# A graph-attention kernel projects raw rows in layer 0, with its loads and its first graph cast reordered

## The chip, the core and the metric

The kernel runs on one core of one Trainium2 chip, as one launch. The metric is the device time in microseconds, shown as the median of several runs. The profile is one execution, recorded by the hardware profiler. Engines are called PE (TensorE), DVE (VectorE), ACT (ScalarE), POOL (GpSimd) and SP (SyncE); SP, ACT and POOL also issue DMAs, each into its own queue.

## The reference

There are two layers, and each adds a graph attention and then a feed-forward part to `x` (3327 rows of 256). Only layer 0's attention is touched by the change; the rest is a mixture of experts, a second attention, and thirty steps of a recurrent block. The attention of layer 0 is, with two heads of 128 columns:

```python
def _L0_gnn_ref(h, adj, W1, b1, W2, b2, W3, b3, a):      # h = layernorm(x)
    W1h = (h @ W1.T + b1).reshape(n, HEADS, C)
    W2h = (h @ W2.T + b2).reshape(n, HEADS, C)
    W3h = (h @ W3.T + b3).reshape(n, HEADS, C)
    a1, a2 = (a[:, :C], a[:, C:])
    s1 = jnp.einsum('nhc,hc->nh', W1h, a1)
    s2 = jnp.einsum('nhc,hc->nh', W2h, a2)
    e = jax.nn.leaky_relu(s1[:, None, :] + s2[None, :, :], ALPHA)
    e = jnp.where(adj[:, :, None] == 1, e, NEG)
    att = jax.nn.softmax(e, axis=1)
    return jnp.einsum('ijh,jhc->ihc', att, W3h).reshape(n, HEADS * C)
```

The graph `adj` is a 3327 x 3327 array of 32-bit integers.

## The kernel before

**Row tiles.** `x` lies in SBUF as 26 tiles of 128 rows. `groups` holds them by four (the last group by two): groups 0 to 6. SP loads one group with each of its first six DMAs of 512 KB (L76), and the last group in three pieces.

**Score weights.** The scores need W1 and W2 only through their products with the attention vector, two columns for each head. These are made once on PE (L415) and copied into the last four columns of `wv`, behind W3 (L419). So one 260-wide product gives both the projection and the scores. The biases' share of the scores, `shift`, comes from two more kinds of small products (L427). W1, W2, the attention vector (`gaT`), the biases and W3 are all loaded by POOL (L400, L412). ACT starts by issuing four DMAs that write zeros into DRAM tables (L393 to L396: `lists`, two rows of `given`, `no_row`).

**Projection.** `project` goes over the groups. For each it takes the statistics of the rows on DVE (L115, L116, L118), the power -1/2 on POOL (L120), and normalizes the rows on DVE (L127, into `xn`). By pairs of tiles, `turned` transposes on PE (L147) and copies to `hT` on ACT (L148); the products with `wv` follow one pair later (L162). `split0` adds the biases (L434, L438) and after each group `Scores.finish` takes three exponentials on ACT (L194 to L196). `project` has a second way, `raw=True`, used by layer 1: rows are turned as they are, the mean is taken out of the weights by `without_mean`, and the factor 1/std is applied to each row's result.

**The graph.** `take_graph` has POOL cast a group of graph rows from integers to one byte each, DRAM to DRAM, into the buffer `in_bytes` (L301), and SP turn them into `adjT` by DMA transposes (L311). `in_bytes` is one buffer, so the next cast waits for these transposes. The first cast is for four row tiles (`groups0[0]`), the later ones for six or four. The kernel places it after the power of group 3:

```python
def first_rows(ts, power):
    nonlocal behind
    behind = power
    if ts is groups[3]:
        take_graph(groups0[0], behind)
```

**Attention.** `attend` walks over parts of row tiles and heads. PE spreads a row factor over the partitions (L221), ACT copies it to `rb` (L225). For each of the 26 neighbour tiles ACT makes `e` (L252), DVE applies the mask to give `pT` (L257), and PE adds the product with `wh` into `acc` (L262).

**Order.** The order of instructions on an engine comes from a scheduler, which follows data dependencies and its own costs. `tc.issue_after(i)` places instructions behind `i`, and `tc.keep_in_program_order` keeps an instruction's place. [...]

Of the kernel before, what the change touches and what calls it, by code (L numbers as in the profile page):

```python
# [11 lines left out]
F32 = mybir.dt.float32  # L12
# [8 lines left out]
P = 128  # L21
# [9 lines left out]
def gat_moe_gat_recurrent_ffn(ctx: ExitStack, tc: tile.TileContext, a: dict, out: bass.AP):  # L31
# [59 lines left out]
            if REST % 2:  # L91
                move(dram[base + REST - 1 : base + REST, :], tile[REST // 2 : REST // 2 + 1, last, :])

    for ts in groups:
        move_pairs(a["x"], x[:, ts[0] : ts[-1] + 1, :], ts[0] // 2, (ts[-1] + 1) // 2, False)

    ident = const.tile([P, P], F32, name="ident")
    make_identity(nc, ident)
# [24 lines left out]
    def normalized(src, dst, scale=1.0):  # L123

        r, mv, power = inverse(src, scale)
        for j in range(len(src)):
            nc.vector.tensor_scalar(  # L127
                dst[j], src[j], mv[:, j, 0:1], r[:, j : j + 1], op0=ALU.subtract, op1=ALU.mult
            )
        return power  # L130

    def without_mean(wv, n_out, ones, p):

        for k in range(KD):
            nc.tensor.matmul(p[:, :n_out], lhsT=ones, rhs=wv[:, k, :], start=(k == 0), stop=(k == KD - 1))
        for k in range(KD):
            nc.vector.scalar_tensor_tensor(
                wv[:, k, :], p[:, :n_out], -1.0 / D, wv[:, k, :], op0=ALU.mult, op1=ALU.add
            )

    def turned(two, work, ps):

# [5 lines left out]
        nc.scalar.copy(hT, pt)  # L148
        return hT

    def project(groups, wv, n_out, finish, work, ps, ps_p, aside, raw=True):

        pending = None

        def products(hT, t, r):
            for j in range(2):
                p = ps_p()  # L160
                for k in range(KD):
                    nc.tensor.matmul(  # L162
                        p[:, :n_out], lhsT=hT[:, j, k, :], rhs=wv[:, k, :], start=(k == 0), stop=(k == KD - 1)
                    )
                finish(t + j, p, *([r[:, j : j + 1]] if raw else []))

        for ts in groups:
            n = len(ts)
            tiles = [x[:, t, :] for t in ts]
            if raw:  # L170
                r, _, power = inverse(tiles)
            else:
                xn = work.tile([P, G, D], F32, name="xn")
                power = normalized(tiles, [xn[:, j, :] for j in range(n)])
            aside(ts, power)
            for j0 in range(0, n, 2):
                hT = turned(x[:, ts[j0] : ts[j0] + 2, :] if raw else xn[:, j0 : j0 + 2, :], work, ps)
                if pending:
                    products(*pending)
                pending = hT, ts[j0], r[:, j0 : j0 + 2] if raw else None  # L180
        products(*pending)

    class Scores:


        def __init__(self, pool, heads, s=None):
            self.s = pool.tile([P, NT, 2, heads], F32, name="s") if s is None else s
            self.row = pool.tile([P, NT, heads], F32, name="row")
            self.full = pool.tile([P, NT, heads], F32, name="full")
            self.part = pool.tile([P, NT, heads], F32, name="part")  # L190
            self.minus = pool.tile([P, NT, heads], F32, name="minus")

        def finish(self, t0, t1):
            nc.scalar.activation(self.full[:, t0:t1], self.s[:, t0:t1, 1], AF.Exp)  # L194
            nc.scalar.activation(self.part[:, t0:t1], self.s[:, t0:t1, 1], AF.Exp, scale=ALPHA)
            nc.scalar.activation(self.row[:, t0:t1], self.s[:, t0:t1, 0], AF.Exp, scale=1.0 - ALPHA)  # L196
            nc.vector.tensor_scalar(self.minus[:, t0:t1], self.part[:, t0:t1], -1.0, None, op0=ALU.mult)

    quick = []
# [158 lines left out]
    with ExitStack() as moe:  # L358
# [17 lines left out]
        C = D // H  # L376
        keep = moe.enter_context(tc.tile_pool(name="keep0", bufs=1))
        wh = keep.tile([P, NT, H, C + 1], F32, name="wh")
        sc = Scores(keep, H)
        ps = moe.enter_context(tc.tile_pool(name="ps0", bufs=4, space=PSUM))  # L380
        ps_o = moe.enter_context(tc.tile_pool(name="ps0o", bufs=2, space=PSUM))
        nc.vector.memset(wh[:, :, :, C : C + 1], 1.0)
# [4 lines left out]
        with ExitStack() as pre:  # L387
            work = pre.enter_context(tc.tile_pool(name="work0", bufs=2))
            hold = pre.enter_context(tc.tile_pool(name="hold0", bufs=1))

            zero = hold.tile([P, E * CAP * 2 // P], F32, name="zero")
            nc.vector.memset(zero, 0.0)
            nc.scalar.dma_start(lists.rearrange("(p n) k -> p (n k)", p=P), zero)  # L393
            for k in range(2):
                nc.scalar.dma_start(given[k * NP + N : (k + 1) * NP, :], zero[: NP - N, :D])
            nc.scalar.dma_start(no_row, zero[:2, : NP // 4])  # L396

            def once(name, shape, src):
                t = hold.tile(shape, F32, name=name)
                nc.gpsimd.dma_start(t, src)  # L400
                return t

            w1 = once("gw1", [P, H, D], a["W1"].rearrange("(h c) d -> c h d", c=P))
            w2 = once("gw2", [P, H, D], a["W2"].rearrange("(h c) d -> c h d", c=P))
            aT = once("gaT", [P, 2, H], a["aT"].rearrange("(s c) h -> c s h", c=P))
            b1 = once("gb1", [P, H], a["b1"])
            b2 = once("gb2", [P, H], a["b2"])
            b3 = once("gb3", [P, D], every_partition(a["b3"], D))


            wv = hold.tile([P, KD, D + 2 * H], F32, name="wv")
            nc.gpsimd.dma_start(wv[:, :, :D], a["W3T"].rearrange("(k p) c -> p k c", p=P))  # L412
            pv = bank()
            for q, (s, h, k) in enumerate((s, h, k) for s in range(2) for h in range(H) for k in range(KD)):
                nc.tensor.matmul(  # L415
                    pv[:, q : q + 1], lhsT=(w1, w2)[s][:, h, k * P : (k + 1) * P], rhs=aT[:, s, h : h + 1],
                    start=True, stop=True,
                )
            nc.vector.tensor_copy(  # L419
                wv[:, :, D:].rearrange("p k q -> p q k"), pv[:, : 2 * H * KD].rearrange("p (q k) -> p q k", k=KD)  # L420
            )
            shift = hold.tile([P, 2, H], F32, name="shift")
            nc.vector.memset(shift, 0.0)
            pv = bank()
            for h in range(H):
                for s, b in ((0, b1), (1, b2)):
                    nc.tensor.matmul(  # L427
                        pv[:, h : h + 1], lhsT=b[:, h : h + 1].to_broadcast([P, P]), rhs=aT[:, s, h : h + 1],
                        start=(s == 0), stop=(s == 1),
                    )  # L430
            nc.vector.tensor_copy(shift[:, 0, :], pv[:, :H])

            def split0(t, p):
                nc.vector.tensor_tensor(  # L434
                    wh[:, t, :, :C], p[:, :D].rearrange("p (h c) -> p h c", h=H),
                    b3.rearrange("p (h c) -> p h c", h=H), ALU.add,
                )
                nc.vector.tensor_tensor(  # L438
                    sc.s[:, t], p[:, D : D + 2 * H].rearrange("p (s h) -> p s h", h=H), shift, ALU.add
                )  # L440
                if t % G == G - 1 or t == NT - 1:
                    sc.finish(t - t % G, t + 1)

            behind = None

            def first_rows(ts, power):
                nonlocal behind
                behind = power  # L450
                if ts is groups[3]:
                    take_graph(groups0[0], behind)

            project(groups, wv, D + 2 * H, split0, work, ps, bank, first_rows, False)
            nc.vector.tensor_scalar(wh[:, NT - 1], wh[:, NT - 1], real[:, 0:1], None, op0=ALU.mult)
            for ts in groups0[1:3]:
                behind = take_graph(ts, behind)


            nc.gpsimd.dma_start(gw, a["gate_w"].rearrange("(k p) e -> p k e", p=P))  # L460
            nc.gpsimd.dma_start(gb[:, 0, :], every_partition(a["gate_b"], E))

            def numbers(dst, pattern, base, step):
                nc.gpsimd.iota(
                    dst, pattern=pattern, base=base, channel_multiplier=step, allow_small_or_imprecise_dtypes=True
                )

            numbers(part, [[0, 1]], 0, 1)
            numbers(rank[:, 0, :], [[-1, E]], E, 0)
            numbers(region[:, 0, :], [[CAP, E]], 0, 0)  # L470
            for k in range(2):
                numbers(pair[:, :, k, 0], [[P, NT]], k * NP, 1)
            nc.gpsimd.affine_select(
                out=before, in_=ones, pattern=[[1, P]], compare_op=ALU.is_gt, fill=0.0, base=0, channel_multiplier=-1
            )
# [620 lines left out]
```

The softmax here doesn't subtract the row's maximum and nothing guards it: scores larger than these inputs give would overflow.

## Time and profile before

| | |
|---|---|
| Median of 3 runs | 1968.25 us (1965.48 to 1968.59) |
| Profiled execution, its own time | 1964.56 us |
| Span in the profile | 1962.6 us |
| Busy: PE / DVE / ACT / POOL | 1908.9 / 1281.6 / 1096.5 / 936.5 us |
| Mean granted PE clock | 0.994 |

The span is the time from the first to the last recorded instruction; the execution's own time holds some 2 us more around it. The busy time of an engine is the sum over its instructions, and a busy PE is not necessarily a PE at its peak rate. In the timeline each row is one instruction or a run of equal ones: start in us, length in us, engine, line, what it writes and reads, and in brackets the idle time of the engine before it, with what ended that. An engine name with a q (SPq, ACTq) is the issue of a DMA.

### The profile page before, as it was taken

What the parts mean: (1) busy time and instruction counts of PE and PEld (TensorE: products, weight loads), DVE (VectorE), ACT (ScalarE), POOL (GpSimd) and SP (SyncE); (2) the same over time, 40 slices, a digit from 0 to 9 for tenths busy, and PEclk for the clock granted to TensorE, in tenths of its full rate; (3) what the DMA queues carried; (4) which work ended last, traced back from release to release, by engine and by line L of the source; (5) the groups of instructions that cost most, each with busy time, mean ns of one, the idle gap of its engine ahead of it and who ended that gap; (6) DMA issues with size and microseconds to landing.
All of it is one profiled execution on the core that took longest, in us unless ns stands there. A gap on an engine that the chain in (4) does not pass through costs nothing.

```text
span 1962.6 us, 33704 instructions
## 1 busy us (share of the span) xinstructions
PE 1908.9 (97%) x12032; PEld 1747.3 (89%) x12032; DVE 1281.6 (65%) x3827; ACT 1096.5 (56%) x1509; POOL 936.5 (48%) x864
## 2 busy tenths in 40 slices
PE   7999999999999997999999999999999999999998
PEld 6999999998999995888888888888888888888887
DVE  6887788832222225566767777777777777777778
ACT  2977766721111113666555666666666666666664
POOL 3020202353333322010000488878888887888886
PEclk9999999999999998999999999999999999999999
DMA  8978051099999874000000000000000000000003
GB/s 168 117 104 118 6 86 50 18 307 303 357 326 336 280 245 148 2 15 9 17 9 17 28 1 1 1 1 1 1 1 1 1 1 1 1 1 1 1 1 118
DMA packets 139756, 157.09 MB, mean 80 GB/s; under 512 B 52028, under 2 KB 99365, under 8 KB 139587
## 3 DMA queue, kind: packets, MB, share of 16 engines
q1 hardware_dynamic: 123466, 122.05, 20.1%
q0 software_dynamic: 11440, 28.09, 8.3%
q10 hardware_dynamic: 4680, 4.76, 0.7%
q8 instruction: 98, 1.61, 0.3%
q14 instruction: 72, 0.58, 0.1%
HBM read 164.58 MB, written 29.78 MB: 99 GB/s over the span
## 4 chain that ended last, share of the span: by engine, by line
PE 71%; issue 9%; POOL 5%; DVE 4%; DMA 3%; ACT 1%; SPq 0%; POOLq 0%; DVEq 0%; ACTq 0%
PE po L1024 35%; PE acc L262 24%; PE pt L1008 8%; POOL given L831 2%; DVE pT L257 2%; POOL rb L730 2%; DMA given<-wh,to 2%; PE bank L786 1%; PE bank L499 1%; DMA wh<-in_w_dram 1%; DMA lists<-pair,ati 1%; DVE x L913 1%; PE bank L221 0%; PE acc L162 0%; ACT zT L1019 0%
## 5 line engine op out<-in xcount | busy, mean ns | idle before, releaser
L1024 PE MATMUL po<-wc,zT 128*128 128x256 f32 x3120 | 700.3, 382 | 3.6 <-ACT zT L1019 3.6
L1024 PEld LDWEIGHTS po<-wc,zT 128*128 128x128 f32 x3120 | 583.0, 190 | 89.0 <-ACT zT L1019 11.2
L1000 POOL TENSOR_TENSOR th<-th,x 128x1024 f32<-128x1024 f32 (+1 forms) x210 | 460.8, 2216 | 120.7 <-ACT th L998 117.9
L252 ACT ACTIVATE e<-rb,minus,full 128x384 f32<-128x384 f32 (+3 forms) x494 | 400.5, 824 | 180.1 <-DVE pT L257 164.1
L257 DVE SCALAR_TENSOR_TENSOR pT<-e,part,adjT 128x384 f32<-128x384 f32 (+3 forms) x494 | 380.5, 774 | 137.5 <-PE acc L262 117.0
L1005 DVE BATCH_NORM_STATS2 stats<-z 128x6 f32<-128x256 f32 x780 | 275.1, 413 | 168.5 <-ACT z L1001 168.5
L1019 ACT COPY zT<-pt 128x512 f32<-128x512 f32 (+1 forms) x300 | 196.7, 721 | 294.1 <-PE pt L1008 294.1
L1030 DVE SCALAR_TENSOR_TENSOR x<-po,rr,bb 128x256 f32<-128x256 f32 x780 | 323.2, 475 | 48.7 <-PE po L1024 42.7
L262 PE MATMUL acc<-wh,pT 128*128 128x129 f32 x2704 | 310.1, 276 | 1.6 <-DVE pT L257 1.6
L262 PEld LDWEIGHTS acc<-wh,pT 128*128 128x128 f32 x2704 | 305.2, 192 | 2.0 <-DVE pT L257 2.0
L262 PE MATMUL acc<-s_wh,pT 128*128 128x257 f32 x1352 | 295.3, 380 | 0.8 <-DVE pT L257 0.7
L262 PEld LDWEIGHTS acc<-s_wh,pT 128*128 128x128 f32 x1352 | 255.9, 190 | 37.7 <-DVE pT L257 1.8
L120 POOL TENSOR_TENSOR rstd<-ve,neg_half 128x4 f32<-128x4 f32 (+3 forms) x28 | 30.4, 1086 | 415.1 <-DVE ve L118 331.5
L989 POOL TENSOR_TENSOR rr<-rr,neg_half 128x4 f32<-128x4 f32 (+1 forms) x210 | 207.2, 989 | 15.0
L1001 ACT ACTIVATE z<-th 128x1024 f32<-128x1024 f32 (+1 forms) x210 | 201.6, 1011 | 0.6 <-POOL th L1000 0.5
L998 ACT ACTIVATE th<-x 128x1024 f32<-128x1024 f32 (+1 forms) x210 | 198.4, 1002 | 0.9 <-DVE x L127 0.9
L1008 PE MATMUL pt<-ident,z 128*128 128x128 f32 x1560 | 189.1, 274 | 2.5 <-DVE high L944 2.5
L1008 PEld LDWEIGHTS pt<-ident,z 128*128 128x128 f32 x1560 | 178.6, 142 | 13.3 <-issue 2.9
L786 PEld LDWEIGHTS bank<-hT,wh 128*128 128x128 f32 x1280 | 149.1, 192 | 5.7 <-issue 3.7
L786 PE MATMUL bank<-hT,wh 128*128 128x128 f32 x1280 | 150.1, 275 | 3.4 <-DMA wh<-in_w_dram 3.4
L820 DVE TENSOR_TENSOR pT<-e,bank 128x512 f32<-128x512 f32 x61 | 41.9, 687 | 165.2 <-PE bank L786 165.1
L816 ACT ACTIVATE e<-bank 128x512 f32<-128x512 f32 x61 | 36.4, 597 | 196.7 <-PE bank L786 184.4
(189 smaller groups left out, 1333.5 us busy)
## 6 DMA issues: line engine op xcount, KB each, us to landing
wh<-in_w_dram SPq DMA_DIRECT2D x120, 512.0 KB
first_set<-in_w_dram SPq DMA_DIRECT2D x63, 512.0 KB
in_bytes<-in_adj_dram POOLq DMA_DIRECT2D x3, 2496.0 KB, 28.7
x<-in_x_dram SPq DMA_DIRECT2D x6, 512.0 KB
kept<-x SPq DMA_DIRECT2D x8, 384.0 KB
old<-kept SPq DMA_DIRECT2D x6, 512.0 KB
out_dram<-x SPq DMA_DIRECT2D x6, 512.0 KB
table_x<-row ACTq DMA_DIRECT2D x3, 768.0 KB
```

The lines of the kernel that those rows point to most:

```text
L252: nc.scalar.activation(e[:, : n * P], rb[:, : n * P], AF.Relu, scale=sc.full[:, j, h : h + 1], bias=sc.minus[:, j, h : h + 1],)
L257: masked = nc.vector.scalar_tensor_tensor(pT[:, : n * P], e[:, : n * P], sc.part[:, j, h : h + 1], adjT[:, j // 2, ts[0] * P : (ts[-1] + 1 ...
L262: nc.tensor.matmul(po[c], lhsT=pT[:, c * P : (c + 1) * P], rhs=wh[:, j, h, :], start=(j == 0 and c % per_bank == 0), stop=(j == NT - 1), s ...
L786: nc.tensor.matmul(p[:, f, :], lhsT=w[:, k, f * P : (f + 1) * P], rhs=hT[:, k, :], start=(k == 0), stop=(k == KD - 1),)
L989: nc.gpsimd.tensor_tensor(r[:, :n], r[:, :n], neg_half[:, :n], ALU.pow)
L998: nc.scalar.activation(th[:, :n, :], hs, AF.Tanh, scale=1.0 / S)
L1000: nc.gpsimd.tensor_tensor(th[:, :n, :], th[:, :n, :], hs, ALU.add)
L1001: nc.scalar.activation(z[:, :n, :], th[:, :n, :], AF.Silu, scale=1.0 / S)
L1005: nc.vector.bn_stats(stats[:, j, :], z[:, j, :])
L1008: nc.tensor.transpose(pt[:, j, k, :], z[:, j, k * P : (k + 1) * P], ident)
L1024: nc.tensor.matmul(po[:, j, :], lhsT=zT[:, j, k, :], rhs=wc[:, k, :], start=(k == 0), stop=(k == KD - 1),)
L1030: nc.vector.scalar_tensor_tensor(x[:, ts[0] + j, :], po[:, j, :], rr[:, j : j + 1], bb, op0=ALU.mult, op1=ALU.add)
```

## The change

Layer 0's projection goes over to raw rows:

- `turned` transposes `x` itself; the 26 normalizing operations are gone. `prepare` now holds the score products and after them `without_mean`, which takes the mean out of all 260 columns of `wv`. `project` calls it once, after two pairs have been turned.
- `split0` multiplies each result by the row's 1/std (`r`) and adds `b3`; the four score columns are multiplied only. The score's bias moves into the exponential of `row`: one ACT operation for each head, with `shift` as its bias.
- The statistics of group 2 and later are placed behind the last instruction of `without_mean`.
- `gaT`, W1 and W2 are issued by ACT as its first instructions. W3 is issued by SP between the first and the second group of `x`. POOL keeps the three bias loads.
- The zeros for DRAM are issued by ACT from within `prepare`, in program order, and no longer at the start.
- The first cast of the graph stands behind the power of group 1 and no longer of group 3.

In the listing of the built program DVE has 3816 instructions instead of 3841, PE 7075 instead of 7073, ACT 1552 instead of 1542, and POOL 882 instead of 886. From the attention on, the streams are the same except for one `rb` copy, which ACT now makes before the first `e` instead of after the eleventh.

```diff
-    for ts in groups:
-        move_pairs(a["x"], x[:, ts[0] : ts[-1] + 1, :], ...)
+    def load_rows(some):
+        for ts in some:
+            move_pairs(a["x"], x[:, ts[0] : ts[-1] + 1, :], ...)
+    load_rows(groups[:1])
...
     def without_mean(wv, n_out, ones, p):
...
-            nc.vector.scalar_tensor_tensor(
+            last = nc.vector.scalar_tensor_tensor(
                 wv[:, k, :], p[:, :n_out], -1.0 / D, wv[:, k, :], op0=ALU.mult, op1=ALU.add
             )
+        return last.ins
...
         for ts in groups:
-            n = len(ts)
-            tiles = [x[:, t, :] for t in ts]
-            if raw:
-                r, _, power = inverse(tiles)
-            else:
-                xn = work.tile([P, G, D], F32, name="xn")
-                power = normalized(tiles, [xn[:, j, :] for j in range(n)])
+            with tc.issue_after(made) if made and ts not in groups[:2] else ExitStack():
+                r, _, power = inverse([x[:, t, :] for t in ts])
             aside(ts, power)
...
+                hT = turned(x[:, ts[j0] : ts[j0] + 2, :], work, ps)
+                if prepare and pending and not made:
+                    made = prepare()
                 if pending:
                     products(*pending)
...
-            nc.scalar.activation(self.row[:, t0:t1], self.s[:, t0:t1, 0], AF.Exp, scale=1.0 - ALPHA)
+                for h in range(self.row.shape[2]):
+                    nc.scalar.activation(
+                        self.row[:, t0:t1, h], self.s[:, t0:t1, 0, h], AF.Exp,
+                        scale=1.0 - ALPHA, bias=self.shift[:, h : h + 1],
+                    )
...
+            nc.sync.dma_start(wv[:, :, :D], a["W3T"].rearrange("(k p) c -> p k c", p=P))
+            load_rows(groups[1:])
+            aT = once(nc.scalar, "gaT", ...)
+            w1 = once(nc.scalar, "gw1", ...)
+            w2 = once(nc.scalar, "gw2", ...)
+            b1 = once(nc.gpsimd, "gb1", [P, H], a["b1"])
+            b2 = once(nc.gpsimd, "gb2", [P, H], a["b2"])
+            b3 = once(nc.gpsimd, "gb3", [P, D], every_partition(a["b3"], D))
...
-            nc.vector.memset(zero, 0.0)
-            nc.scalar.dma_start(lists.rearrange("(p n) k -> p (n k)", p=P), zero)
-            for k in range(2):
-                nc.scalar.dma_start(given[k * NP + N : (k + 1) * NP, :], zero[: NP - N, :D])
-            nc.scalar.dma_start(no_row, zero[:2, : NP // 4])
...
-                nc.gpsimd.dma_start(t, src)
...
-            nc.gpsimd.dma_start(wv[:, :, :D], a["W3T"]...)
...
+            def prepare():
+                pv = bank()
...
+                nc.vector.tensor_copy(wv[:, :, D:]..., pv[:, : 2 * H * KD]...)
+                last = without_mean(wv, D + 2 * H, ones, bank())
+                pv = bank()
...
+                nc.vector.tensor_scalar(shift, pv[:, :H], 1.0 - ALPHA, None, op0=ALU.mult)
+                nc.vector.memset(zero, 0.0)
+                for dst, src in zeros:
+                    tc.keep_in_program_order(nc.scalar.dma_start(dst, src))
+                return last
...
-                nc.vector.tensor_tensor(wh[:, t, :, :C], p[:, :D]..., b3..., ALU.add)
-                nc.vector.tensor_tensor(sc.s[:, t], p[:, D : D + 2 * H]..., shift, ALU.add)
+                nc.vector.scalar_tensor_tensor(
+                    wh[:, t, :, :C], p[:, :D]..., r, b3..., op0=ALU.mult, op1=ALU.add)
+                nc.vector.tensor_scalar(sc.s[:, t], p[:, D : D + 2 * H]..., r, None, op0=ALU.mult)
...
-                if ts is groups[3]:
+                if ts is groups[1]:
                     take_graph(groups0[0], behind)
...
-            project(groups, wv, D + 2 * H, split0, work, ps, bank, first_rows, False)
+            project(groups, wv, D + 2 * H, split0, work, ps, bank, first_rows, prepare)
```

## The prediction

> **What bounds the kernel now.** I first read the page's chain of waits: the run is TensorE's from end to end.
>
> ```profile
> PE 71%; issue 9%; POOL 5%; DVE 4%; DMA 3%; ACT 1%; SPq 0%; POOLq 0%; DVEq 0%; ACTq 0%
> ```
>
> From the first attention product on, the built programs of both kernels hold the same instructions in the same order on all engines, bar one ACT copy. So I took the start (0 to 60 us) from the timeline in order of time; columns are start, length, engine, line, operation, count, and in brackets the idle time before and what ended it.
>
> ```profile
> 0.81 11.90 SPq L76 DMA_DIRECT2D x<-in_x_dram  x9
> 2.37 0.37 ACTq L393 DMA_DIRECT2D lists<-zero  x1
> 11.84 3.54 PE L415 MATMUL bank<-gaT,gw 128*128 128x1 f32 x16 [11.84 <-DMA gaT<-in_aT_dram]
> 16.08 1.01 POOL L120 TENSOR_TENSOR rstd<-ve,neg_half 128x4 f32<-128x4 f32 x1 [0.63 <-DVE ve L118]
> 17.04 0.91 POOL L301 DMA_DIRECT2D in_bytes<-in_adj_dram  x1
> 19.29 0.23 POOL L464 IOTA part<- 128x1 f32 x1
> 20.06 3.20 PE L162 MATMUL bank<-wv,hT 128*128 128x260 f32 x8
> 25.73 1.92 PE L162 MATMUL bank<-wv,hT 128*128 128x260 f32 x8
> 36.17 7.69 SPq L311 DMA_TRANSPOSE adjT<-in_bytes  x4
> ```
>
> TensorE stands until the score weights land (11.84). The first projection product is at 20.06; from the third pair of row tiles (25.73) a pair takes 2.19 us (27.92 less 25.73), all of it TensorE's. The stage's end, in the same columns:
>
> ```profile
> 47.39 0.77 POOL L301 DMA_DIRECT2D in_bytes<-in_adj_dram  x1 [16.98 <-DMA adjT<-in_bytes]
> 48.97 3.29 PE L221 MATMUL bank<-ident,row 128*128 128x128 f32 x28
> 50.15 0.58 ACT L225 COPY rb<-bank 128x512 f32<-128x512 f32 x1
> 51.61 7.29 DVE L257 SCALAR_TENSOR_TENSOR pT<-e,part,adjT 128x512 f32<-128x512 f32 x9 [1.41 <-ACT e L252]
> ```
>
> The first graph group is transposed by 47.39 (its buffer is free then), the masks start at 51.61 behind ACT, the products (L262) at 52.42, and TensorE is then busy 25.84 of the 26 us from 50 to 76. So what moves 52.42 moves the end; a vector or DMA saving before it alone does not.
>
> **The queues.** The DMA view by stretches of 2 us gives packets, MB and share of the 16 engines. From 8 to 10 us, with the loads of POOL (q0), ACT (q10) and SP (q1):
>
> ```profile
> q0 software_dynamic: 103, 0.31, 38.7%
> q10 hardware_dynamic: 98, 0.30, 36.8%
> q1 hardware_dynamic: 110, 0.20, 26.3%
> ```
>
> From 14 to 16, `x` alone:
>
> ```profile
> q1 hardware_dynamic: 323, 0.59, 98.5%
> ```
>
> and from 20 to 22, the graph's cast alone:
>
> ```profile
> q0 software_dynamic: 63, 0.21, 102.9%
> ```
>
> So 2 us on 16 engines over the packets: an `x` packet of 2 KB takes 0.10 us, a cast packet 0.51.
>
> [...] 103, 98 and 110 packets side by side. So an `x` packet beside the cast has to wait 0.51 us for each turn. [...] the cast stays in POOL's queue, behind POOL's other work (17.04 follows 16.08 + 1.01). [...] eight passes take 3.20 us at 20.06 and 1.92 at 25.73. I keep that loss after the change as it was, ±1 us.
>
> **The change, part by part.**
>
> *Normalized rows go.* 26 L127 operations (407 ns each, 10.6 us of DVE) fall away; 26 additions L434 (420 ns) become scalar_tensor_tensor from PSUM (475 ns in L1030): +1.4 us of DVE. All this is beside TensorE's 2.19 us a pair; from 20 to 24 TensorE is busy 4.00 of 4.00. The saving counts only in that products need no normalizing.
>
> *Loads.* W1, W2 and the attention vector go from POOL (issues of 0.98, 0.77 and 0.74 us) to ACT's queue, with no wait; W3 goes behind the first `x` group on SP. Ahead of the second `x` group and the score weights lie 512 (`x`) + 256 (W3) + 512 (W1, W2) + 512 (`x`) + 128 (b3) KB = 1.97 MB. The trace moved 0.52, 0.60 and 0.70 MB in 2 to 4, 4 to 6 and 6 to 8 us, and 0.81 in the next; so they are through at 8.4, and land some 0.75 later (512 KB were through at 4.0, first statistics at 4.75): 9.15.
>
> *Score products and mean.* 3.54 us of products from 9.15: 12.7; then copy to `wv` (0.16), two more products (about 0.9 cold), two 260-wide corrections on DVE (0.8), with some 1 us of hand-overs: 15.5 by this path.
>
> *A hidden order.* In the built program DVE has two small copies of `part` (`vec`) between the `wv` copy and the corrections, and they wait for POOL's IOTA, which comes after the cast. Second group lands 9.15; statistics took 1.98 to the start of `ve` (4.75 to 6.73): 11.13; the power starts 0.25 later and takes 1.04: 12.42; the cast's issue, two gate DMAs and the IOTA took 17.04 to 19.52, 2.48: 14.9. Two copies (0.2) and the corrections (0.8) then give 15.9, the first product 16.1 to 16.7. This path ends last: I take 16.4, against 20.06: **-3.7 us**.
>
> *Zeroing DMAs move into ACT's stream* between the second and third `hT` copy. [...] in the built program these wait in order for W2, for `x` groups 2 and 4 (counted from 0), and the last for `x` group 5. The third `hT` copy and all later ACT work queue behind. The third pair would be due at 16.4 + 5.7 = 22.1 (20.06 to 25.73 before), its copy at 21. Group 5 needs 4 more loads of 1.6 us after 8.4 plus 1.1 for `lists`: through at 15.9, landed 16.7, **0 us**, if the cast is not yet moving. I expect so: issue ends 13.3, and a queue that starts beside a busy SP queue has been slow (lists issued 2.37, W1 1.61, and from 4 to 6 us only q1 moved), against 0.7 on a quiet chip. That puts the first cast packet at about 16.8, the bounds being 14.0 and 17.5.
>
> *Cast earlier.* It takes 17.5 us from first packet to transposes, then 11.2 (36.17 to 47.39): ready at 46 with a start at 16.8. Products need it 4 us before 52.42 at most. Covered; it caps the gain at some 5.5 us.
>
> *ACT's end.* Built ACT has two `rb` copies ahead of the first `e` (+0.58), and one more exponential (+0.1): **+0.7 us**, on the path, since TensorE has only 0.2 us idle before 52.42.
>
> *The wait of later statistics on the corrections* delays only groups 2 on, which have DVE time: about 21 us of work in 29.
>
> Sum: -3.7 + 0 + 0.7 = **-3.0 us**, from the profiled 1964.56 (span 1962.6) to 1961.6. That execution lies 3.7 under the median 1968.25 of three runs (1965.48 to 1968.59), so I say 1965.2 for a median.
>
> **Rivals.**
>
> *Starvation (slower).* The cast's packets come in before group 5 has passed; each remaining `x` packet then costs 0.51 + 0.10 us, group 5 has 16 per DMA engine, and ACT stands on it with the third `hT`. First cast packet at 14.0 with 16 left: 9.8 us, landed 24.6, third pair 25.7, no gain and +0.7. Each packet more adds 0.6: from 22 left (cast at 13.4) it is slower by over 0.2%, and 25 left, a cast at 13.1, give +6: 1974. For it: the equal counts above. Against: the slow start of a second queue under load. 17%.
>
> *Weights late (no change).* ACT's queue is quiet until 6 to 7 us as with `lists`. The weights land near 13, first product about 19.2: -0.9 + 0.7, about 1968. For: L393's 4.6 us. Against: ACT issues at the same moment as SP, with nothing moving. 15%.
>
> *Loads quicker, or a warm TensorE (faster).* Landing at 7.7 gives a first product at 14.9 and -4.5; a warm clock another -1: 1963. Capped by the transposes. 30%.
>
> *The stated case*, with those near it: 38%. It would be no change if another wait held 52.42, the transposes for one.
>
> **How the numbers follow.** About 0.2%, 3.9 us, is what a measurement of this kernel can tell from no change. The stated case and late weights lie within it, 53% together; the quicker start gives 30% for faster, starvation 17% for slower. The range: 1961 is a gain of 7, beyond the cap by the spread of runs; 1972 is starvation at 22 packets. I leave out some 5% below and 12% above. The likeliest case alone is 1963.5 to 1967.5.
>
> **What would show it.** Right: L415's counterpart starts near 9, the cast's issue near 12.4, the first 128x260 `wv,hT` product at 16 to 17, no ACT gap ahead of the third `hT` that ends on a DMA, mask start near 48.6. Wrong: an ACT gap up to 24 us or later ahead of `no_row` (starvation), score products after 12 (late weights), or a mask start that a DMA releases. Any change past the first attention part would also refute the reading.

## The result, and the profile after

The changed kernel takes 1965.39 us (median of 20 runs) against 1968.49 us for the kernel before (20 runs on the same chip). The ratio is 0.9983, with a 95% interval of 0.9977 to 0.9989: **3.3 us faster**, between 2.2 and 4.5. A second set of runs, beside which the kernel before took 1964.27 us, gave 0.9984 (0.9977 to 0.9990).

The timeline of the changed kernel's start, in the columns of the prediction (start, length, engine, line, operation, count, and in brackets the idle time before and what ended it). L167 is the projection's product (L162 before), L429 the score products (L415 before):

```profile
6.71 1.83 PE L429 MATMUL bank<-gaT,gw 128*128 128x1 f32 x8
10.13 1.86 PE L429 MATMUL bank<-gaT,gw 128*128 128x1 f32 x8 [1.58 <-DMA gw<-in_W_dram]
12.25 2.10 PE L138 MATMUL bank<-wv,ones 128*128 128x260 f32 x4 [0.26 <-DVE wv L433]
12.38 0.72 POOL L312 DMA_DIRECT2D in_bytes<-in_adj_dram  x1
14.14 1.71 PE L440 MATMUL bank<-gaT,gb 128*128 128x1 f32 x8
14.44 0.15 POOL L481 IOTA part<- 128x1 f32 x1
14.76 0.76 DVE L140 SCALAR_TENSOR_TENSOR wv<-bank,wv 128x260 f32<-128x260 f32 x2
15.71 3.81 PE L167 MATMUL bank<-wv,hT 128*128 128x260 f32 x8
16.01 0.23 ACTq L447 DMA_DIRECT2D no_row<-zero  x1
19.32 1.06 PE L151 MATMUL bank<-ident,x 128*128 128x128 f32 x4
22.47 1.92 PE L167 MATMUL bank<-wv,hT 128*128 128x260 f32 x8
```

W1's score products run before W2 has landed (6.71), W2's at 10.13. The first projection product starts at 15.71 instead of 20.06, 4.35 earlier. Only 3.26 of that is left at the third pair (22.47 against 25.73), since the first pair now takes 3.81 instead of 3.20. (A pair of about 2 us is called warm here and one of 3.2 to 3.9 us cold; the words stand for these lengths alone.) The stage's end, same view:

```profile
43.77 0.77 POOL L312 DMA_DIRECT2D in_bytes<-in_adj_dram  x1 [6.85 <-DMA adjT<-in_bytes]
47.14 1.14 ACT L236 COPY rb<-bank 128x512 f32<-128x512 f32 x2
49.03 18.90 DVE L268 SCALAR_TENSOR_TENSOR pT<-e,part,adjT 128x512 f32<-128x512 f32 x22 [1.96 <-ACT e L263]
49.84 20.37 PE L273 MATMUL acc<-wh,pT 128*128 128x129 f32 x180 [0.83 <-DVE pT L268]
```

The first attention product moves from 52.42 to 49.84, **2.58 us earlier**, and the masks still start behind ACT, not behind a DMA. The transposed graph is there at 43.77, 5.3 us before it is needed.

The DMA queues from 14 to 16 us (packets, MB, share of the 16 engines; q10 is ACT's queue, q1 SP's, q0 POOL's):

```profile
q10 hardware_dynamic: 134, 0.39, 48.5%
q1 hardware_dynamic: 196, 0.34, 45.3%
q0 software_dynamic: 8, 0.03, 12.8%
```

The cast's first 8 packets move at the end of this stretch, and from 16 to 18 us only 24 packets of `x` are left: the cast came when `x` had nearly passed.

This profiled execution took 1968.48 us (span 1966.8), at the upper end of its runs. From the first attention product to the end it took 1917.0 us, where a profile from the second set, with that product at 49.87, took 1906.9, and the kernel before 1910.2. The two are still within 0.4 us of each other at the first product of the expert stage (341.8 and 341.5 us after the first attention product), so the loss came later. The first profile serves for the start alone.

### The profile page after: what moved, and what is told of

Its sections match the earlier page's. It is cut to its first block, busy times and chain, and to the rows that moved or that the text cites. A ratio compares the mean times of both kernels' runs of the same rounds, so it can differ in the third digit from the quotient of the medians.

```text
span 1966.8 us, 33692 instructions
## 1 busy us (share of the span) xinstructions
PE 1915.8 (97%) x12036; PEld 1751.4 (89%) x12036; DVE 1277.1 (65%) x3802; ACT 1098.6 (56%) x1516; POOL 936.0 (48%) x860
## 4 chain that ended last, share of the span: by engine, by line
PE 85%; DVE 5%; issue 4%; POOL 2%; DMA 2%; ACT 1%; SPq 0%; ACTq 0%; another core or an unknown queue 0%; POOLq 0%; DVEq 0%
PE po L1041 35%; PE acc L273 26%; PE pt L1025 8%; PE bank L803 8%; PE acc L844 3%; DVE pT L268 2%; PE bank L167 1%; POOL given L848 1%; PE bank L151 1%; POOL rb L747 1%; PE bank L516 1%; POOL rstd L123 1%; PE bank L232 0%; DVE x L930 0%; PE acc L794 0%
```

## The experiments

Each was timed beside the kernel before on its own chip, where that took 1963.15 to 1964.27 us; so ratios are compared, not absolute times. The changed kernel itself was repeated on one of these chips and is there at 0.9984.

**A repeat of the changed kernel** (after_again), without an edit.

> The changed kernel unchanged, for a second profile of its later stages. Theory: first attention product at 49.8 again, and the 5 us that the first profile of it lost in the expert stage are one execution's own: from the first attention product to the end about 1908 to 1911 us, as in the other kernels, against 1916.9; own time near 1960 to 1965 beside the kernel before of the same chip. Rival (the change itself costs time in the expert stage): 1916 again.

Measured: 1960.42 us, ratio 0.9984 (0.9977 to 0.9990); first attention product at 49.87, 1906.9 us from there to the end. The loss of the first profile does not come back; it is not the change's.

**The cast back behind group 3** (u1_cast_late).

```diff
-                if ts is groups[1]:
+                if ts is groups[3]:
```

> The changed kernel with one part undone: the first graph cast stands behind the power of group 3 again. My theory: raw rows and the new loads only bring the first attention product forward because the transposed graph is there in time; with the cast behind group 3 it is issued near 28.5 us (group 3's statistics now stand behind the corrected weights), is through its transposes near 58, and the first attention product waits for it until about 58.5 instead of 49.84. So the time is about 8.7 us above the changed kernel, near 1974. Rival (the cast's place does not matter, the first pairs alone set the stage): first attention product at 49.8, time 1965.

Measured: 1971.94 us, ratio 1.0039 (1.0026 to 1.0052). Timeline:

```profile
59.51 2.08 DVE L268 SCALAR_TENSOR_TENSOR pT<-e,part,adjT 128x512 f32<-128x512 f32 x3 [11.95 <-DMA adjT<-in_bytes]
60.32 4.03 PE L273 MATMUL acc<-wh,pT 128*128 128x129 f32 x17 [10.82 <-DVE pT L268]
```

A row of the table by stretches (length, busy PE, granted clock, DMA share, GB/s):

```profile
60.00:62.00 2.00, 1.68 (x8) 0.50 0.63 25
```

The masks wait 11.95 us for the transposed graph, and TensorE stands with them. The first attention product is 10.5 us later than with the early cast. The cast is issued at 28.96 here and not at 17.04 as in the kernel before, since group 3's statistics now stand behind the corrected weights. So the cast has to move with the rest: left behind group 3, it turns the change's gain into a loss. The earlier cast alone, in the kernel before, was not run; there the masks wait for ACT and not for the graph. The first expert product comes 345.7 us after the first attention product, where the repeat has 341.5. Part of that is a lower granted clock: after TensorE's 10.82 us of idle time it is 0.50 in the row above, and 0.86 on average from 60 to 80 us, where the repeat has 1.00. By estimate that is up to 2.8 us (0.14 of 20) of the 4.2.

**The loads back, raw rows kept** (u2_loads_back).

```diff
-    load_rows(groups[:1])
+    load_rows(groups)
...
-            nc.sync.dma_start(wv[:, :, :D], a["W3T"]...)
-            load_rows(groups[1:])
-            aT = once(nc.scalar, "gaT", ...)
-            w1 = once(nc.scalar, "gw1", ...)
-            w2 = once(nc.scalar, "gw2", ...)
+            w1 = once(nc.gpsimd, "gw1", ...)
+            w2 = once(nc.gpsimd, "gw2", ...)
+            aT = once(nc.gpsimd, "gaT", ...)
...
+            nc.gpsimd.dma_start(wv[:, :, :D], a["W3T"]...)
...
+            nc.vector.memset(zero, 0.0)
+            for dst, src in zeros:
+                nc.scalar.dma_start(dst, src)
...
-                nc.vector.memset(zero, 0.0)
-                for dst, src in zeros:
-                    tc.keep_in_program_order(nc.scalar.dma_start(dst, src))
```

> The changed kernel with all loads and zeroing DMAs issued as in the kernel before (score weights by POOL, zeros first on ACT, W3 behind them); raw rows and the earlier cast stay. My theory: the early landing of the score weights is what raw rows need; the weights land near 11.8 again, score products take to 15.4, the corrections come after, first projection product near 18.8, third pair near 25.5, first attention product near 52.9 with ACT's +0.7, and the time is 1968 to 1969, no gain on the kernel before. Rival (raw rows alone bring the gain, as the normalizing of group 0 and 1 no longer stands ahead of the first product): first product near 16.5, first attention product near 50.3, time 1966.

Measured: 1964.38 us, ratio 1.0003 (0.9995 to 1.0012). Timeline (L442 are the bias products, L440 in the change):

```profile
17.23 1.70 PE L442 MATMUL bank<-gaT,gb 128*128 128x1 f32 x8
18.79 3.81 PE L167 MATMUL bank<-wv,hT 128*128 128x260 f32 x8
```

The weights land at 11.53, the first product is at 18.79, the first attention product at 53.32: **raw rows without the new loads gain nothing**. The first product does come 1.27 us earlier than in the kernel before. That is gone by the third pair (25.68 against 25.73), since the first pair takes 3.81 us instead of 3.20, the transposes behind it 1.06 instead of 0.60, and the second pair 2.15 instead of 1.92; ACT's longer tail (27.64 us from the third pair, against 26.69 in the kernel before) then makes it a small loss at the first attention product.

**The normalized rows back, new loads kept** (u3_norm_back).

It was built from the kernel before, and the edit is shown against that one:

```diff
-    for ts in groups:
-        move_pairs(a["x"], x[:, ts[0] : ts[-1] + 1, :], ...)
+    def load_rows(some):
...
+    load_rows(groups[:1])
...
+            nc.sync.dma_start(wv[:, :, :D], a["W3T"]...)
+            load_rows(groups[1:])
+            aT = once(nc.scalar, "gaT", ...)
+            w1 = once(nc.scalar, "gw1", ...)
+            w2 = once(nc.scalar, "gw2", ...)
...
-                if ts is groups[3]:
+                if ts is groups[1]:
```

> The kernel before with the changed kernel's loads (score weights first on ACT, W3 on SP behind group 0, zeros on ACT behind the weights) and its earlier cast, but with normalized rows and the old score bias. My theory: the copy of the score columns to the weights stands in VectorE's order inside or behind the normalizing, which takes the rows of groups 0 and 1 first, so an early landing of the weights alone gives little: first product near 19.5 to 20, first attention product near 52, time 1968 to 1969. Rival (the earlier loads alone bring the gain): first product near 16, first attention product 48.5 to 49, time 1965.

Measured: 1963.69 us, ratio 1.0001 (0.9993 to 1.0009); first product at 19.69, first attention product at 53.12. Timeline:

```profile
11.90 0.17 DVE L422 COPY wv<-bank 128x8 f32<-128x8 f32 x1 [6.23 <-PE bank L418]
16.27 1.94 DVE L130 TENSOR_SCALAR xn<-x,mv,rstd 128x256 f32<-128x256 f32 x5
16.73 0.69 PE L150 MATMUL bank<-ident,xn 128*128 128x128 f32 x2 [4.44 <-DVE xn L130]
```

The outcome fits, the reason that I had given does not. The copy of the score columns is not behind the normalizing but far ahead of it: it stands in VectorE's order after group 0's first statistics, and VectorE stands 6.23 us on the score products, whose second half waits for W2 (10.00). Only then (11.90) come the rest of the statistics, of further groups too, and the first normalizing is at 16.27. TensorE waits 4.44 us for it. So here the rows are late because of where the copy stands; an order with the normalizing ahead of the copy was not run. As built, **neither half of the change gains alone**: in one kernel the weights end the wait for the first product, in the other the rows, at 18.79 and 19.69.

**The cast one group earlier** (e4_cast_early).

```diff
-                if ts is groups[1]:
+                if ts is groups[0]:
```

> The changed kernel with the first graph cast one group earlier still, behind the power of group 0. Starvation theory: the cast's first packet moves near 12 us with some 26 packets of x left on each DMA engine, each of which then costs 0.51 + 0.10 us; group 5 lands near 29, ACT stands on the last zeroing DMA until then, the third pair of projection products is near 31 instead of 22.5, and the time about 1974. Rival (the queues do not disturb each other that much, or the cast starts late under load wherever it is issued): third pair at 22.5, transposed graph earlier than 43.8, time 1965 or a little below.

Measured: 1974.46 us, ratio 1.0047 (1.0034 to 1.0060). The queues from 14 to 16 us:

```profile
q0 software_dynamic: 45, 0.15, 71.9%
q10 hardware_dynamic: 45, 0.15, 18.4%
q1 hardware_dynamic: 48, 0.10, 14.4%
```

And the timeline:

```profile
32.29 0.23 ACTq L447 DMA_DIRECT2D no_row<-zero  x1
32.62 1.07 ACT L152 COPY hT<-bank 128x512 f32<-128x512 f32 x2 [25.07 <-DMA x<-in_x_dram]
33.26 3.84 PE L167 MATMUL bank<-wv,hT 128*128 128x260 f32 x8 [10.22 <-ACT hT L152]
```

This is starvation as the prediction had it as a rival: three queues with nearly equal counts (45, 45 and 48 packets), `x` down to an eighth of its rate (48 packets in 2 us, against 384 from 12 to 14 us in the change), ACT standing on the last zeroing DMA until 32.29, and TensorE on ACT for 10.22 us. The first pair after this standstill is a cold one once more, with 3.84 us. The cast's issue came 4.5 us earlier than in the change (7.92 against 12.38); that turns 3 us of gain into 9 us of loss.

**The early cast with the zeros later** (e5_zero_late).

```diff
-                for dst, src in zeros:
-                    tc.keep_in_program_order(nc.scalar.dma_start(dst, src))
...
-                if ts is groups[1]:
+                if ts is groups[0]:
...
             project(groups, wv, D + 2 * H, split0, work, ps, bank, first_rows, prepare)
...
+            for dst, src in zeros:
+                tc.keep_in_program_order(nc.scalar.dma_start(dst, src))
```

> The kernel with the cast behind group 0's power, and the four zeroing DMAs issued by ACT after the projection instead of inside it. It tells apart two ways in which the early cast cost 10 us. Theory (the lane, not the data): x needs its groups only every 4.4 us, so the slowed loads are still in time, and what hurt was ACT standing on the last zeroing DMA until group 5 had landed; with the zeros later, third pair near 22.5 and first attention product near 49.9 again, time within 1.5 us of the changed kernel's. Rival (the rows themselves come too late for the projection): a gap in the projection's pairs that ends on an x load, first attention product 53 or later, 1969 or more.

Measured: 1995.66 us, ratio 1.0158 (1.0144 to 1.0172). For the question it was built for, the theory held nearly: third pair at 22.18, with the cast as early as in the last experiment. The slowed rows are late for the projection once only: VectorE waits for `x` until 31.13, and two pairs are 3.05 us apart there instead of 2.19. What cost in the last experiment was the place of ACT's `hT` copies behind the last zeroing DMA: that was issued at 32.29, the next two copies started at 32.62. But the forecast of the time was wrong by over 30 us. Timeline:

```profile
31.13 0.43 DVE L118 BATCH_NORM_STATS2 st<-x 128x6 f32<-128x256 f32 x1 [1.79 <-DMA x<-in_x_dram]
47.53 28.81 ACTq L471 DMA_DIRECT2D given<-zero  x2
78.62 1.07 ACT L236 COPY rb<-bank 128x512 f32<-128x512 f32 x2 [30.82 <-DMA adjT<-in_bytes]
```

At their new place the issues of the two `given` DMAs stretch over 28.81 us, the last zeroing DMA is issued at 78.35, and the `rb` copies behind it start at 78.62; the trace puts ACT's 30.82 us of idle time down to graph transposes, which SP issues until 83.53 (31.42 + 52.11). It is the picture of the last experiment with another holder: there it was an `x` load, with 25.07 us. Why the issues wait for just these DMAs is not shown. In both runs ACT's work behind a small DMA started only after it, and a large DMA ended the wait.

**A warm TensorE** (e6_warm). Three dense products, whose results are not used, in the gap ahead of the first pair, and the bias products (L440 in the change) ahead of W2's score products. The second part only changes the order and is not shown.

```diff
+                spare = bank()
+                for _ in range(3):
+                    tc.keep_in_program_order(nc.tensor.matmul(
+                        spare[:, :D], lhsT=ident, rhs=x[:, 0, :], start=True, stop=True
+                    ))
```

> The changed kernel with three dense 128x256 products on TensorE in the gap ahead of the first projection product (their results are not used), and the score bias products moved ahead of the second weight's score products. It measures the cold clock, which the prediction carried as +-1 us. Theory: [...] the first pair takes 2 instead of 3.81 us and the transposes and the second pair are short as well; third pair near 20 instead of 22.5, first attention product near 47.5, the time 2 us or more below the changed kernel. Rival (the single-column products count as work already[...]): first pair 3.8 us again, time as the changed kernel.

Measured: 1959.38 us, ratio 0.9976 (0.9969 to 0.9982); first attention product at 47.92, 1.95 earlier than in the repeat. Timeline:

```profile
14.12 2.23 PE L456 MATMUL bank<-x,ident 128*128 128x256 f32 x6
16.18 1.92 PE L167 MATMUL bank<-wv,hT 128*128 128x260 f32 x8
17.93 0.60 PE L151 MATMUL bank<-ident,x 128*128 128x128 f32 x4
```

The first product comes 0.5 us later than in the change, behind the added products, and yet the third pair 1.9 earlier (20.56): the pairs take 1.92 from the start, and the transposes 0.60 instead of 1.06. **The cold start cost 2.5 us** (the first pair's 1.9, and 0.6 in the transposes and the second pair: 1.06 and 2.18 in the repeat, 0.60 and 1.92 here). The median is only 1.04 below the repeat's, and the two intervals overlap; so the gain at 48 us is shown, and how much of it reaches the end is not. In this one profile 1.7 us are gone by the first expert product: from 180 to 200 us TensorE is busy 18.52 us in both, but the granted clock is 0.91 here and 1.00 in the repeat.

**W2 on SP, early IOTA, dense products and late zeros** (b1_best).

```diff
+            w2 = once(nc.sync, "gw2", [P, H, D], a["W2"]...)
             nc.sync.dma_start(wv[:, :, :D], a["W3T"]...)
...
+        tc.keep_in_program_order(nc.gpsimd.iota(part, ...))
         rank = route_p.tile([P, 1, E], F32, name="rank")
...
+                both = hold.tile([P, 2, H], F32, name="both")
+                for s, b in ((0, b1), (1, b2)):
+                    nc.vector.tensor_tensor(both[:, s, :], b, aT[:, s, :], ALU.mult)
...
+                for s in range(2):
+                    tc.keep_in_program_order(nc.tensor.matmul(pv[:, :H], lhsT=ones, rhs=both[:, s, :], ...))
...
```

> The changed kernel with four additions: W2 issued by SP ahead of W3, the IOTA of the partition numbers at POOL's start, the dense products ahead of the first pair, with the bias products as two of two columns, and the zeroing DMAs after the projection. Theory: W2 lands near 7.5, the corrections no longer wait for POOL, and the corrected weights stand near 14.3; first product near 14.5 (15.71), third pair near 18.8, first attention product near 46.3, 3.5 us below the changed kernel. Rival (the first graph group's transposes then set the start of the masks, as they land near 44): first attention product 48 or later, 1 to 2 us below the changed kernel.

Measured: 1995.84 us, ratio 1.0166 (1.0152 to 1.0180). It has the late zeros, and with them ACT stands 32.28 us until transposes end it, as in e5_zero_late (first attention product at 82.11). Its first pair took 2.00 us and its third pair was at 20.52. What the other additions are worth at the first attention product does not show in it; the next kernel has the zeros where the change has them.

**The same with the zeros where the change has them, and one dense product instead of three** (c2_best).

> The changed kernel with three additions: W2 issued by SP ahead of W3, the IOTA of the partition numbers at POOL's start, and the bias products as two of two columns on the column sums, with one dense 128x256 product more ahead of the first projection product. The zeroing DMAs stay where the change put them. Theory: score products done near 10, their copy near 11.6 behind group 1's statistics, corrected weights at 14.8, first product near 15, warm from the first or the second pair on: third pair near 19.5 instead of 22.5, first attention product near 46.9, time 3 us below the changed kernel. Rival (the transposed graph, landed near 44, becomes the wait): first attention product 48 or later.

Measured: 1958.78 us, ratio 0.9976 (0.9970 to 0.9983); third pair at 20.78, first attention product at 48.14. The weights' earlier landing came to nothing. Timeline:

```profile
10.29 0.75 DVE L118 BATCH_NORM_STATS2 st<-x 128x6 f32<-128x256 f32 x2 [3.42 <-DMA x<-in_x_dram]
12.29 0.17 DVE L436 COPY wv<-bank 128x8 f32<-128x8 f32 x1
```

The score products are through at 10.17 instead of 11.99, but in VectorE's order their copy stands behind group 1's statistics, which wait for rows that now land after W2 (10.29). The copy is at 12.29, 0.26 later than in the change. Its first product is at 16.11, later than in the change, but the first pair takes 2.20 us instead of 3.81: what this kernel gains is the shorter first pair, as e6_warm does.

**The second `rb` copy later** (c1_tail).

```diff
-                    following = row_factors(*parts[k + 1])
+                    with tc.issue_after(made.ins) if leave and not k else ExitStack():
+                        following = row_factors(*parts[k + 1])
...
-                nc.scalar.activation(
+                made = nc.scalar.activation(
```

> The changed kernel with one ACT instruction moved: the second rb copy stands behind the twelfth e again, as in the kernel before, and no longer ahead of the first. It tests the prediction's ACT tail of +0.7 us. Theory: from the third projection pair to the first attention product 26.8 us instead of 27.4, first attention product near 49.25, the time 0.5 us lower, too little for the timing alone. Rival (the tail is set by something else, TensorE's row-factor products or a DMA): 27.4 and 49.85 as before the edit.

Measured: 1959.85 us, ratio 0.9988 (0.9979 to 0.9998); first attention product at 49.38. Timeline:

```profile
47.13 0.56 ACT L236 COPY rb<-bank 128x512 f32<-128x512 f32 x1
```

From the third pair (22.46) to the first attention product 26.92 us, against 27.37 with the copy ahead: the copy was worth 0.45. The timing alone cannot show that, as expected.

**Both** (c3_both), the last two edits in one kernel.

> The two edits together: the later second rb copy, and the three additions (W2 on SP, early IOTA, narrow bias products with a dense product behind them). Theory: first attention product near 46.3, time 3.5 us below the changed kernel and some 6 to 7 below the kernel before. Rival (the transposed graph or the second product of the masks is the wait by then): as the three additions alone, or 48 and later.

Measured: 1959.14 us, ratio 0.9978 (0.9968 to 0.9988); first attention product at 48.38, third pair at 21.46. Its first pair took 3.40 us, where the kernel without the later copy took 2.20 with the same instructions ahead of it: one dense product did not shorten the first pair equally in both. With three the first pair took 1.92 and 2.00 us in two runs; with none, and the single-column bias products there, 3.80 or 3.81 in seven. The medians of c2_best, c3_both and e6_warm lie 4.0 to 4.9 us below the kernel before, and their ratios 0.6 to 0.8 thousandths below the changed kernel's, with overlapping intervals. They beat the kernel before; that they beat the changed kernel is likely, not shown.

## Why the prediction was right, and where not

The forecast was 1965.2 from a sum of -3.0 us; measured were 1965.39 and -3.3 (2.2 to 4.5). The reading that the first attention product sets the time held. It moved by -2.58 us, and over all twelve timings of the changed kernel and its variants the time against the kernel before moves with it: within 0.8 us in the nine that moved it by up to 8 us, and 9.2 for 10.7, 31.0 for 32.2 and 32.6 for 29.7 us in the others. That the total was met to 0.3 us is in part luck: the measurement itself is uncertain by more than 1 us, and two steps on the way to the first product were mis-sized and offset each other. Point by point:

- **Landing.** Group 1's rows were predicted at 9.15 and its first statistics start at 9.37. But W2 landed only with the products at 10.13, 1 us later than assumed; that W1's products had been done before it gave it back (score products through at 11.99, against 12.7).
- **The hidden order did not decide.** POOL's IOTA was predicted at 14.9 and came at 14.44, the corrections follow at 14.76 as described. But the first product did not wait for it. In the cast experiments the corrections start earlier (14.47 with the late cast, 14.51 with the early one, there behind the mean products L138 and no longer behind POOL), and the first product comes no earlier (15.79 and 15.83). What stands directly ahead of it in TensorE's order are the bias products L440, four of them in eight passes: 14.14 + 1.71 = 15.85, and the product starts at 15.71. In the late-cast run the same sum is 15.93 against 15.79, in the early-cast run 15.98 against 15.83, in the repeat 15.70 against 15.61. With the loads back, where POOL's IOTA is done long before, it is 18.93 against 18.79. No run leaves the place ahead of the first product empty, so this is read from the lines. **The prediction's path left these 1.7 us out**. It also put the mean products L138 at 0.9 us, where they take 2.10 (its own line of the kernel before, eight cold passes in 3.20 us, gives an estimate of 1.6 for four). It came within 0.7 us of the start because another wait of nearly the same end was put in their place, and because half of the score products ran while W2 was still on its way.
- **The cold start** was carried as unchanged, within 1 us. It was the term that moved: the first pair lengthened by 0.6 us, and 1.1 of the 4.35 us gained at the first product was lost by the third pair. So the first product came 0.65 us earlier than predicted and the cold pairs took 1.1 back; by that luck the third pair is near its forecast: predicted -3.7, measured -3.26.
- **ACT's end**: +0.7 predicted, 0.68 measured (3.26 less 2.58), of which the later `rb` copy accounts for 0.45.
- **The zeroing DMAs**: what each of them waits for was the author's reading of the built program. The trace has the first issued at 10.16, when W2's products start (10.13), and the two of `given` at 10.98 and 13.69. Group 5 was predicted to land at 16.7, and the last of them was issued at 16.01, before the third `hT` copy was due. The trace puts 12.97 us of that copy's wait down to `no_row`; that name is wrong, since its transposes only end at 20.38; in the repeat the same wait, 12.89, is put down to the transposes. The cost was zero, by a margin that the early cast shows to be thin.
- **The cast**: issue predicted near 12.4, measured 12.38; first packet predicted at 16.8, measured between 15.2 and 15.4, within the bounds; transposes through at 43.8, predicted 46. Starvation was priced right in kind. One cast packet for each `x` packet was the author's estimate, from the 103, 98 and 110 packets side by side; the early cast has 45 and 48 of them from 14 to 16 us, and 107 and 109 from 20 to 24. In size, 26 packets at 0.61 us, and 0.75 to land, would by that estimate have ended near 29; measured 32.3. The zeros in ACT's queue moved beside them (45 packets from 14 to 16 us), but their packets come to only about 1.1 us for each DMA engine from 12 to 33 us (5.1% of it), so the rest of the difference is open.

## What to carry to other kernels

When two preparations end close together, costing one of them at a time gives no gain for either, as here (ratios 1.0003 and 1.0001); list every instruction that stands ahead of the first useful one in its engine's order, the small ones too, price them from a row that follows a standstill if TensorE has stood before (here 3.81 us against 1.92 for a pair), and take the latest. A load that is moved forward does not help if the consumer's place in the order stays: here, with W2 on SP, the score products were done 1.8 us earlier and their copy came 0.26 later (c2_best). Before a DMA is moved in an engine's order, find out what its issue will wait for there: in e4_cast_early and e5_zero_late such an issue held ACT up for 25.07 and 30.82 us. Three dense products in a gap ahead of a dense stage brought the first attention product 1.95 us forward (e6_warm).

## What was not expected of the hardware

- Single-column fp32 products did not make the first pair warm here. In the change TensorE is busy for 1.71 us from 14.14 on with L440's 128x1 products, after 2.10 us of 260-wide ones, and the first pair still takes 3.81 us. With 2.23 us of 256-wide products in the same gap it takes 1.92 (e6_warm).
- The granted clock in the profile does not show the cold start: the table by stretches has 1.00 for both kernels from 12 to 24 us, while a pair takes 3.20 and 3.81 us. Later in a run it did show one, 0.50 from 60 to 62 us after the standstill of u1_cast_late. For the start of these kernels the durations of equal rows are what to read.
- A cast issued early started late. From issue to first packet it took about 2.9 us in the change (12.38 to between 15.2 and 15.4) and 4.0 with the early cast (7.92 to between 11.9 and 12.0), both while `x` was moving at full rate (384 packets from 12 to 14 us, 422 from 10 to 12), against some 1.6 in the kernel before (17.04 to between 18.6 and 18.8), where few `x` packets were left (64 from 16 to 18). With the normalized rows back it was also short (16.30 to between 17.6 and 17.8), though `x` was still moving (222 packets from 16 to 18); so load on SP's queue alone does not explain it, and the cause is open.
